# A decoder layer: the first half's attention weights stored by groups of 128 queries, and score copies shared between two engines

## The chip, the cores and the metric

The kernel runs on one core of a Trainium2 chip. The metric is the device time of one execution in microseconds (us). Three executions of the kernel before took 1036.89, 1038.47 and 1040.36 us, so its median is 1038.47 us. Besides these there is one profiled execution, which gives the page and the trace.

Engine names in the profile: PE is TensorE's matmul side and PEld its weight loads, DVE is VectorE, ACT is ScalarE, POOL is GpSimd, SP is SyncE. A name with q behind it (SPq, ACTq) is an engine's sequencer, which here issues transfers.

## The reference

The layer works on x of shape (8, 512, 256) in float32: eight batches of 512 tokens. Three blocks follow each other, each with a residual sum and a layer norm behind it.

```python
x = _layernorm(x + _L0_attn_ref(x, ...))              # windowed attention, 16 heads of 16
x = _layernorm(x + _L0_xattn_ref(x, ctx_1024, ctx_1024))  # causal cross-attention, one head
x = _layernorm(x + _L0_ffn_ref(x, ...))               # 8 experts, the best 2 for each token
```

The change lies in the first block. There each token looks at 17 keys, from 8 before it to 8 behind it, and a soft mask made from a learned width and sharpness is taken off the scores:

```python
q = _ln(silu(x @ Wq).reshape(B, L, H, D), q_g, q_b)
kv = silu(x @ Wkv)                      # k gets the same norm as q, v does not
scores = stack([einsum('blhd,blhd->blh', q, k_pad[:, w:w + L]) for w in range(K)]) * SCALE
soft_mask = sigmoid((width[..., None] - rel) * sharp[..., None])
attn = softmax(scores - (1.0 - soft_mask) * MASK_PENALTY, axis=-1)
out = sum(attn[..., w][..., None] * v_pad[:, w:w + L] for w in range(K))
```

## The kernel before, in words

**Stages.** Generators, one for each stage of a batch, are interleaved by `together` (L1110), which gives every stage a share of the iteration by costs and due times written in the code. In iteration b (L1132) the stages are `crossed(b)` (cross-attention and routing), `attended(b + 1)` (the end of the windowed attention), `scores(b + 2)` (its start) and, from iteration 1 on, some experts' tiles of 128 tokens each. A batch therefore passes through `scores`, then `attended`, then `crossed`, in three successive iterations. The first experts' tile comes in iteration 1, and the tiles that are left follow after the last batch.

**Order on the queues.** The SP queue runs its transfers in the order in which the code issues them (L83). On PE, DVE, ACT and POOL the order is planned when the kernel is built, from a model of each instruction's time; at run time each engine takes its instructions strictly in that order, and one that waits holds back all that stand behind it.

**Scores.** In `scores` (L305) q and k of one batch are computed, normed and transposed. The heads are handled in two halves, c = 0 and c = 1, of 8 heads each, and for each half in two steps `ip` of 256 queries. A step makes four tiles `pq[r]` of 128x320 numbers in PSUM from 32 small matmuls (L413): each block of 64 queries against a span of 80 keys, two heads in each of the four. The four tiles take all four buffers of their pool, so the next step's matmuls wait until they are copied out. The copies (L421) go to a tile `row` with two buffers, all four by ACT, and ACT then issues two transfers (L425) that store `row` to the DRAM array `band[c]`. The array's lines are so spaced that what is stored as blocks of 80 keys can be read back as diagonals of 17: POOL reads them into the tile `s[c]` (L387) once all stores of that half have landed.

**Weights and sums of the first three batches.** Batches below BANDED = 3 end in `summed` (L496), the others in `weighted` (L610), which uses no matmul for the sums. In `summed` DVE takes the mask off, subtracts the maximum and, after ACT's exponential, divides by the sum (L518 to L533), for c = 0 and then c = 1. Here partition p holds the queries 4p to 4p + 3. SP stores the weights of a half in one transfer, `aband<-s` (L537): 128 partitions x 4 queries x 4 pairs of heads, each a run of 34 numbers or 136 bytes. The array is laid out so that a block of 64 queries can be read back as a banded matrix over 80 keys. After the store of c = 0 SP issues the first two of eight `fetch` calls (L502), each of which reads one group g of 128 queries in two transfers `arow<-aband` (L506); the tile `arow` has two buffers. Then comes the store of c = 1, and the other six fetches follow inside the loop over groups (L567). PE transposes each `arow` (L575), DVE and ACT copy the result out as `aT` (L579), and small matmuls (L553) with the values sum it.

**What SP has behind a store.** In the iterations concerned these are the fetches, the store of the other half, the loads of x and of the context of later batches (L91, L919), and in iteration 1 the first experts' tile, whose rows `xs` (L942) come ahead of the store of batch 2 and whose weights were issued earlier still.

Of the kernel before, what the change touches and what calls it, by code (L numbers as in the profile page):

```python
# [14 lines left out]
P = 128  # L15
# [5 lines left out]
W = 17  # L21
# [4 lines left out]
HG = HH // 2  # L26
LINE = HG * SPAN * 2
HALO = W // 2
T = L // P
# [8 lines left out]
BANDED = 3  # L38
# [6 lines left out]
def decoder_layer_kernel(  # L45
# [16 lines left out]
    nc = tc.nc  # L62
# [242 lines left out]
    def scores(b, xb):  # L305
# [78 lines left out]
        def read_scores(c):  # L384
            lines = band[c].rearrange("(p t n) -> p t n", p=P, t=T)[:, :, 0:LINE]
            read.append(
                nc.gpsimd.dma_start(  # L387
                    s[c].rearrange("p t r w u -> p t r (w u)"),
                    lines.rearrange("p t (r n) -> p t r n", r=HG)[:, :, :, 0 : 2 * W],
                )  # L390
            )
# [9 lines left out]
        for c in range(2):  # L401
            s.append(apool.tile([P, T, HG, W, 2], F32, tag="s", name="s", bufs=3))
            for ip in range(T // 2):
                row = apool.tile([P, 2, HG, SPAN, 2], F32, tag="row", name="row", bufs=2)
                pq = [
                    ps_m.tile([P, 2, SPAN, 2], F32, tag="m", name=f"pq{r}") for r in range(HG)
                ]
                for ii in range(2):
                    for u in range(2):
                        at = (2 * ip + ii) * P + u * QB  # L410
                        for r in range(HG):
                            rs = slice(32 * r, 32 * r + 32)
                            nc.tensor.matmul(  # L413
                                pq[r][u * QB : (u + 1) * QB, ii],
                                qT[rs, c, at : at + QB],
                                kT[rs, c, :, at : at + SPAN].rearrange("p u k -> p k u"),
                                start=True,
                                stop=True,
                            )
                for r in range(HG):  # L420
                    nc.scalar.copy(row[:, :, r], pq[r])  # L421
                to = band[c].rearrange("(b n) -> b n", b=L // QB)[:, 0 : QB * LINE]
                to = to.rearrange("(i u) (p n) -> u p i n", u=2, n=LINE)
                for u in range(2):
                    nc.scalar.dma_start(  # L425
                        to[u, :, 2 * ip : 2 * ip + 2],
                        row[u * QB : (u + 1) * QB].rearrange("p i r k u -> p i (r k u)"),
                    )
                yield 2.0

                if c == 1 and ip == 0:
                    read_scores(0)
# [48 lines left out]
        for c in range(2):  # L481
            pc = pen[:, c].rearrange("p t r w u -> p (t r) w u")
            wc = width[:, c].rearrange("p t (r u) -> p (t r) u", u=2)
            sc = sharp[:, c].rearrange("p t (r u) -> p (t r) u", u=2)
# [11 lines left out]
    def summed(b):  # L496


        groups = [(c, g) for c in range(2) for g in range(T)]
        rows_of = {}  # L500

        def fetch(c, g):  # L502
            ar = apool.tile([P, HG, SPAN, 2], F32, tag="a", name="arow", bufs=2)
            for u in range(2):
                ub = (g * P + u * QB) * (LINE + 2)
                nc.sync.dma_start(  # L506
                    ar[u * QB : (u + 1) * QB].rearrange("p r k u -> p (r k u)"),
                    aband[c][ub : ub + QB * LINE].rearrange("(p n) -> p n", p=QB),
                )
            rows_of[c, g] = ar  # L510

        s, pen, vh = out_of.pop(b)
        for c in range(2):
            sc = s[c]


            with tc.issue_after(urgent[-1].ins) if urgent and c == 0 else nullcontext():
                nc.vector.scalar_tensor_tensor(  # L518
                    sc, pen[:, c], -4.0e4, sc, ALU.mult, ALU.add
                )  # L520
            flat = sc.rearrange("p t r w u -> p (t r) w u")
            byw = sc.rearrange("p t r w u -> p (t r) u w")
            full = [P, T * HG, W, 2]
            top = spool.tile([P, T * HG, 2], F32, tag="top", name="top")
            nc.vector.tensor_reduce(top, byw, AX.X, ALU.max)
            nc.vector.tensor_tensor(
                flat, flat, top[:, :, None, :].to_broadcast(full), ALU.subtract
            )
            nc.scalar.activation(sc, sc, AF.Exp, scale=0.25)
            den = spool.tile([P, T * HG, 2], F32, tag="den", name="den")  # L530
            nc.vector.tensor_reduce(den, byw, AX.X, ALU.add)
            nc.vector.reciprocal(den, den)
            nc.vector.tensor_tensor(  # L533
                flat, flat, den[:, :, None, :].to_broadcast(full), ALU.mult
            )
            lines = aband[c].rearrange("(p t n) -> p t n", p=P, t=T)[:, :, 0:LINE]
            nc.sync.dma_start(  # L537
                lines.rearrange("p t (r n) -> p t r n", r=HG)[:, :, :, 0 : 2 * W],
                sc.rearrange("p t r w u -> p t r (w u)"),
            )  # L540
            if c == 0:

                for early in groups[:2]:
                    fetch(*early)
            yield 5.0
        oT = apool.tile([P, KC, L], F32, tag="T", name="oT", bufs=4)
        aT = apool.tile([P, 2, HG, 2, P], F32, tag="prod", name="aT")

        def sums(c, g):
            po = ps_o.tile([P, 2, 2, QB], F32, tag="o", name="pw")  # L550
            for u in range(2):
                for r in range(HG):
                    nc.tensor.matmul(  # L553
                        po[32 * r : 32 * r + 32, u],
                        vh[c][0:SPAN, 2 * g + u, 32 * r : 32 * r + 32],
                        aT[0:SPAN, g % 2, r, :, u * QB : (u + 1) * QB],
                        start=True,
                        stop=True,
                    )

            to = oT[:, c, g * P : (g + 1) * P].rearrange("c (u q) -> c u q", u=2)
            nc.scalar.mul(to, po[:, :, 0, :], par[:, 0:1])
            nc.vector.scalar_tensor_tensor(
                to, po[:, :, 1, :], par[:, 1:2], to, ALU.mult, ALU.add
            )

        for k, (c, g) in enumerate(groups):  # L567
            if 2 <= k + 1 < len(groups):
                fetch(*groups[k + 1])
            ar = rows_of.pop((c, g))  # L570
            for i in range(2):
                pt = ps_h.tile([P, 2, 2, P], F32, tag="h", name="paT")
                for r in range(2):
                    for u in range(2):
                        nc.tensor.transpose(  # L575
                            pt[0:SPAN, r, u, :], ar[:, 2 * i + r, :, u], ident
                        )
                put = nc.scalar.copy if i else nc.vector.tensor_copy
                put(aT[0:SPAN, g % 2, 2 * i : 2 * i + 2], pt[0:SPAN])  # L579
            if k:  # L580
                sums(*groups[k - 1])
            yield 1.4
        sums(*groups[-1])
        yield 0.8
        return oT
# [546 lines left out]
    for b in range(-2, B + 1):  # L1132
        streams = [(fetched(b), 1.0, 0.45, 1.0)] if b > -2 else []
        if 0 <= b < B:
            streams.append((crossed(b), 31.0, 0.0, 0.93))
        if 0 <= b + 1 < B:
            streams.append((attended(b + 1, rows[b + 1][:, :, 0:E]), 29.4 if b + 1 < BANDED else 60.0, 0.08, 1.0))
        if b + 2 < B:
            streams.append((scores(b + 2, rows[b + 2][:, :, 0:E]), 38.0, 0.0, 0.88))
        m = max(0, -((NX * (TS - 1) - 2 * L * b) // TS)) if b < B else tiles_max  # L1140
        if m > had:
            streams.append((experts(m - had, b == B), (m - had) * 7.2, 0.0, 1.0))
            had = m
        together(*streams)
# [57 lines left out]
```

## Time and profile before

| what | value |
|---|---|
| executions | 1036.89, 1038.47, 1040.36 us |
| profiled execution, its time | 1045.55 us |
| profiled execution, its span | 1043.8 us |
| PE busy | 916.5 us (88%) |
| DVE busy | 627.4 us (60%) |
| ACT busy | 556.7 us (53%) |
| POOL busy | 251.5 us (24%) |
| mean granted TensorE clock | 0.913 |
| `aband<-s` (L537) | 6 transfers of 272 KB, at 57.8 to 220.0 us |
| `arow<-aband` (L506) | 48 transfers of 160 KB, at 67.2 to 245.2 us |
| copies `row<-pq` (L421) | 128, of 432 ns median |

All times inside an execution are counted from the start of its span. The profiled execution is 0.7% longer than the median of the three. The work that the change touches lies between 37 and 245 us: the scores of batches 0, 1 and 2 begin at about 30, 92 and 165 us, and their weights are stored from 57.8, 124.7 and 210.1 us on. PE was at work for 80% or less of many slices there and for 90% or more of nearly every slice after 300 us. A busy matmul engine is not an engine at its peak, since the durations of matmuls grow where the granted clock is low.

### The profile page before, as it was taken

What the parts mean: (1) busy time and instruction counts of PE and PEld (TensorE: products, weight loads), DVE (VectorE), ACT (ScalarE), POOL (GpSimd) and SP (SyncE); (2) the same over time, 40 slices, a digit from 0 to 9 for tenths busy, and PEclk for the clock granted to TensorE, in tenths of its full rate; (3) what the DMA queues carried; (4) which work ended last, traced back from release to release, by engine and by line L of the source; (5) the groups of instructions that cost most, each with busy time, mean ns of one, the idle gap of its engine ahead of it and who ended that gap; (6) DMA issues with size and microseconds to landing.
All of it is one profiled execution on the core that took longest, in us unless ns stands there. A gap on an engine that the chain in (4) does not pass through costs nothing. (4 is left out here: it accounts for less than half of the span.)

```text
span 1043.8 us, 18932 instructions
## 1 busy us (share of the span) xinstructions
PE 916.5 (88%) x6336; PEld 761.6 (73%) x6336; DVE 627.4 (60%) x2106; ACT 556.7 (53%) x978; POOL 251.5 (24%) x211
## 2 busy tenths in 40 slices
PE   5658879868979999999999999999999989999970
PEld 3435557546858777777888778887998988999960
DVE  5164654754489969979994989489953331111106
ACT  4556746656467556658755865576355311222224
POOL 1100100400232243125212522152241241121221
PEclk9677877867799989999999999999999999999995
DMA  9574563872699788689978896898898899999949
GB/s 205 137 124 135 115 153 81 227 164 64 185 319 311 239 267 271 198 257 337 282 206 268 309 292 184 234 364 292 264 279 256 272 260 372 314 337 323 330 116 320
DMA packets 129123, 252.09 MB, mean 242 GB/s; under 512 B 29536, under 2 KB 76704, under 8 KB 127744
## 3 DMA queue, kind: packets, MB, share of 16 engines
q1 hardware_dynamic: 89312, 183.30, 54.3%
q0 software_dynamic: 17824, 41.86, 16.2%
q10 hardware_dynamic: 21888, 25.70, 9.0%
q8 instruction: 52, 0.85, 0.3%
q14 instruction: 47, 0.39, 0.1%
HBM read 193.44 MB, written 57.36 MB: 240 GB/s over the span
## 5 line engine op out<-in xcount | busy, mean ns | idle before, releaser
L1011 PEld LDWEIGHTS ph<-xsT,w1h 128*128 128x128 f32 x2176 | 264.6, 196 | 14.2 <-issue 5.2
L1011 PE MATMUL ph<-xsT,w1h 128*128 128x128 f32 x2176 | 271.6, 280 | 2.9 <-DVE xsT L1000 2.8
L1028 PE MATMUL pf<-w2h,h 128*128 128x256 f32 x1088 | 255.9, 386 | 3.2 <-ACT h L1019 3.1
L1028 PEld LDWEIGHTS pf<-w2h,h 128*128 128x128 f32 x1088 | 204.1, 194 | 32.0 <-ACT h L1019 5.7
L1037 POOL DMA_INDIRECT total<-ye,toi x68 | 120.4, 1771 | 417.0 <-ACT ye L1036 117.0
L1019 ACT ACTIVATE h<-ph 128x512 f32<-128x512 f32 x136 | 81.2, 598 | 119.0 <-PE ph L1011 115.0
L1000 DVE COPY xsT<-pxs 128x256 f32<-128x256 f32 x68 | 28.7, 423 | 174.6 <-PE pxs L997 174.6
L651 DVE TENSOR_TENSOR prod<-prod 128x1024 f32<-128x1024 f32 (+3 forms) x160 | 104.1, 651 | 0.3
L1036 ACT ACTIVATE ye<-pf,g 128x256 f32<-128x256 f32 x68 | 32.2, 473 | 127.2 <-PE pf L1028 116.7
L643 DVE TENSOR_TENSOR prod<-vhalo,a 128x2176 f32<-128x2176 f32 x40 | 96.6, 2416 | 0.2
L815 POOL DMA_INDIRECT sorted_x<-xr,to x64 | 78.2, 1222 | 19.9 <-issue 17.1
L413 PE MATMUL pq<-kT,qT 32*64 32x160 f32 x1024 | 60.3, 391 | 19.2 <-ACT row L421 12.7
L387 POOL DMA_DIRECT2D s<-band x16 | 24.3, 1520 | 214.5 <-DMA band<-row 154.5
L321 PE MATMUL pa<-wall,xT 128*128 128x512 f32 x128 | 67.5, 615 | 6.0 <-ACT qk L323 4.7
L413 PEld LDWEIGHTS pq<-kT,qT 32*64 32x64 f32 x1024 | 37.2, 156 | 33.8 <-ACT row L421 18.1
L421 ACT COPY row<-pq 128x320 f32<-128x320 f32 x128 | 45.8, 435 | 29.4 <-PE pq L413 26.6
L575 PE MATMUL paT<-ident,arow 128*80 128x128 f32 x192 | 38.0, 346 | 20.0 <-DMA arow<-aband 17.1
L1019 ACT ACT_TABLE_LOAD x39 | 50.0, 1283 | 7.3 <-PE ph L1011 5.7
L322 PEld LDWEIGHTS pb<-wall,xT 128*128 128x128 f32 x128 | 24.2, 192 | 35.3 <-issue 23.0
L575 PEld LDWEIGHTS paT<-ident,arow 128*80 128x80 f32 x192 | 26.2, 167 | 30.8 <-issue 13.0
L711 PE MATMUL ps<-cT,x1T 128*128 128x128 f32 (+3 forms) x128 | 45.5, 476 | 0.0
L322 PE MATMUL pb<-wall,xT 128*128 128x288 f32 x128 | 41.3, 410 | 3.9 <-DVE wp L325 1.6
(196 smaller groups left out, 1392.4 us busy)
## 6 DMA issues: line engine op xcount, KB each, us to landing
w1h<-in_w_dram SPq DMA_DIRECT2D x136, 512.0 KB
w2h<-in_w_dram SPq DMA_DIRECT2D x136, 512.0 KB
band<-row ACTq DMA_DIRECT2D x64, 320.0 KB
vhalo<-vband POOLq DMA_DIRECT2D x10, 1280.0 KB, 10.1
xs<-sorted_x SPq DMA_DIRECT2D x68, 132.5 KB
arow<-aband SPq DMA_DIRECT2D x48, 160.0 KB
s<-band POOLq DMA_DIRECT2D x16, 272.0 KB, 5.8
xr<-in_x_dram SPq DMA_DIRECT2D x8, 512.0 KB
```

Source lines behind the costliest of these rows:

```text
L321: nc.tensor.matmul(pa, lhs, wall[:, kc, 0 : 2 * E], **se)
L322: turns.append(nc.tensor.matmul(pb, lhs, wall[:, kc, 2 * E :], **se))
L413: nc.tensor.matmul(pq[r][u * QB : (u + 1) * QB, ii], qT[rs, c, at : at + QB], kT[rs, c, :, at : at + SPAN].rearrange("p u k -> p k u"), st ...
L421: nc.scalar.copy(row[:, :, r], pq[r])
L575: nc.tensor.transpose(pt[0:SPAN, r, u, :], ar[:, 2 * i + r, :, u], ident)
L643: nc.vector.tensor_tensor(prod.rearrange("p w (h d) -> p w h d", d=D), vh[c][:, t : t + W, :].rearrange("p w (h d) -> p w h d", d=D), a[:, ...
L651: nc.vector.tensor_tensor(prod[:, 0:n, :], prod[:, 0:n, :], prod[:, n : 2 * n, :], ALU.add)
L815: sent = nc.gpsimd.indirect_dma_start(out=sorted_x[:, :], out_offset=bass.IndirectOffsetOnAxis(ap=to[:, n, j : j + 1], axis=0), in_=xr[:, ...
L1011: nc.tensor.matmul(ph[:, u, :], w1s[hf][:, kc, f * P : (f + 1) * P], xT[:, kc, :], start=(kc == 0), stop=(kc == KC - 1),)
L1019: nc.scalar.activation(h, ph, AF.Gelu)
L1028: nc.tensor.matmul(po, hs[fc // HU][:, fc % HU, j * P : (j + 1) * P], w2s[hf][:, f, :], start=(fc == 0), stop=(fc == NF - 1),)
L1037: add = nc.gpsimd.indirect_dma_start(out=total[:, :], out_offset=bass.IndirectOffsetOnAxis(ap=toi[:, j : j + 1], axis=0), in_=y, in_offset ...
```

## The change

Two places change.

In `scores`, for the batches 0, 1 and 2, the copies of `pq[1]` and `pq[3]` are made by DVE and those of `pq[0]` and `pq[2]` stay with ACT. The later batches keep all four on ACT.

In `summed`, the store of the weights for c = 0 is cut along the partitions into four transfers, each of 32 partitions, that is of 128 consecutive queries, so that each holds what one `fetch` reads. They are issued one after the other on SP, ahead of the first two fetches. The store for c = 1 stays one transfer. The number of runs and of bytes is the same.

```diff
                 for r in range(HG):
-                    nc.scalar.copy(row[:, :, r], pq[r])
+                    put = nc.vector.tensor_copy if b < BANDED and r % 2 else nc.scalar.copy
+                    put(row[:, :, r], pq[r])
...
             lines = aband[c].rearrange("(p t n) -> p t n", p=P, t=T)[:, :, 0:LINE]
-            nc.sync.dma_start(
-                lines.rearrange("p t (r n) -> p t r n", r=HG)[:, :, :, 0 : 2 * W],
-                sc.rearrange("p t r w u -> p t r (w u)"),
-            )
+
+            parts = T if c == 0 else 1
+            for ps in (slice(k * P // parts, (k + 1) * P // parts) for k in range(parts)):
+                nc.sync.dma_start(
+                    lines[ps].rearrange("p t (r n) -> p t r n", r=HG)[:, :, :, 0 : 2 * W],
+                    sc[ps].rearrange("p t r w u -> p t r (w u)"),
+                )
```

## The prediction, made before the result was known

> **What bounds the kernel now.** I read the page's head and slices first, then busy time by stretches, then the waits of PE and SP from 28 to 262 us, then the order of time around the stores. The page:
>
> ```profile
> PE 916.5 (88%) x6336; PEld 761.6 (73%) x6336; DVE 627.4 (60%) x2106; ACT 556.7 (53%) x978; POOL 251.5 (24%) x211
> PE   5658879868979999999999999999999989999970
> PEclk9677877867799989999999999999999999999995
> ```
>
> A slice is 26 us. From the twelfth on PE is nearly full. The first ten slices, where all that is changed lies, have idle PE and a low clock. So PE sets the end, and an idle microsecond taken from PE early moves all later work forward. By stretches (busy us of PE, PEld, DVE, ACT, POOL, then clock, DMA share, GB/s):
>
> ```profile
> 28.00:110.00 82.00, 57.63 (x517) 38.07 (x516) 32.19 (x61) 46.73 (x89) 8.10 (x8) 0.71 0.60 132
> ...
> 63.50:71.00 7.50, 0.04 (x1) 0.07 (x2) 4.32 (x8) 3.33 (x5) 0.00 (x0) 0.75 0.42 113
> ...
> 131.00:136.00 5.00, 0.15 (x2) 0.02 (x1) 0.54 (x1) 2.35 (x4) 0.00 (x0) 0.61 0.83 234
> 136.00:142.00 6.00, 5.78 (x26) 3.52 (x26) 2.01 (x6) 0.46 (x2) 0.00 (x0) 0.50 0.88 97
> ```
>
> Two stretches have no PE work at all. The waits name them (us in total, times, longest):
>
> ```profile
> PE paT L575 <- DMA arow<-aband: 17.1, 4, 7.5
> PE pq L413 <- ACT row L421: 9.1, 5, 4.8
> ```
>
> ```profile
> SPq L506 <- DMA aband<-s: 25.9, 5, 8.7
> ```
>
> PE waits for fetched weights, and SP holds the fetch until the store has landed. Batch 0 in order of time:
>
> ```profile
> 57.83 0.60 SPq L537 DMA_DIRECT2D aband<-s  x1
> ...
> 67.16 0.72 DVE L533 TENSOR_TENSOR s<-s,den 128x544 f32<-128x544 f32 x1
> 67.19 2.44 SPq L506 DMA_DIRECT2D arow<-aband  x4
> 69.80 0.63 SPq L537 DMA_DIRECT2D aband<-s  x1
> 70.93 1.50 PEld L575 LDWEIGHTS paT<-ident,arow 128*80 128x80 f32 x8 [7.92 <-DMA arow<-aband]
> 70.96 1.91 PE L575 MATMUL paT<-ident,arow 128*80 128x128 f32 x8 [7.49 <-DMA arow<-aband]
> ```
>
> The store goes out at 57.83, the fetch at 67.19, the transposes start at 70.96: 9.36 us of landing are the largest piece. The same rows put the store at 124.72 and the fetch at 131.26 in batch 1 (6.54 us, PE stall 4.85), and 210.12 and 217.51 in batch 2 (7.39 us, stall 3.08).
>
> **The change, part by part: the stores.** One transfer of 128 x 4 x 4 = 2048 runs of 136 bytes becomes four of 512. No row before shows such a quarter. The nearest is the store `wband<-wp`, 64 KB in 512 runs of 128 bytes: issued at 73.66 it lets POOL go on at 80.65 (7.0 us), at 138.70 by 144.45 (5.75), at 217.54 by 220.98 (3.44). Those are the bounds, 3.44 to 7.0. I take a line through the least of each size (512 runs 3.44, 2048 runs 6.54): 2.41 us fixed, and the rest in proportion to runs. The quarter then lands after 2.41 + (9.36 - 2.41)/4 = 4.15 us in batch 0, 3.44 in batch 1, 3.66 in batch 2, and the fetch may go 5.2, 3.1 and 3.7 us sooner. SP now issues four transfers of 0.63 us, 2.52 us in all, still under 3.44, so the landing hides the three added issues (9 in all, 5.7 us of SP). Without that cover each batch would pay up to 1.9 us. Behind them SP holds only fetches, the store of c = 1 and loads for later batches.
>
> What becomes of it on PE:
> - Batch 0: the first stall can lose 5.2 of 7.49, but group 2 is late next. Its fetch comes behind the store of c = 1, whose data are ready at 67.16 + 0.72 = 67.88 and which goes at 69.80 only because SP was issuing fetches. It can move 1.9 us, no more. The stall ahead of group 2 (1.71 us at 79.88 now) takes the rest back. I count 1.9; the other end is 5.2.
> - Batch 1: 3.1 of the 4.85. Group 2's transposes at 146.02 did not wait for a transfer, so nothing takes it back.
> - Batch 2: the stall is 3.08 and the fetch comes 3.7 sooner: 3.1. The store itself stays behind the load of `xs` on SP (209.67), which the change does not touch.
>
> Sum 8.1. With the quarter at 7.0 us it would be 1.9 + 0 + 0.4 = 2.3; at the other end 5.2 + 3.1 + 3.1 = 11.4.
>
> **The copies.** 3 batches x 2 halves x 2 steps x 2 = 24 copies leave ACT (24 x 0.432 = 10.4 us) for DVE. The trace has no DVE copy of 128x320 from PSUM. 128x256 takes 0.42 (L1000) and 80x512 takes 0.69 (L579), so by interpolation 0.49, 11.8 us in all. DVE is busy 121 of the 234 us there, so this lies beside other work unless a copy is awaited. Per step, four copies on ACT take 1.41 us; now ACT's pair (0.75) and DVE's pair (0.98) run side by side: 0.43 less. The next 32 matmuls, held by these copies, took 2.33 and where not held 1.92 (165.29): 0.41 less. On the path lies one such sum per batch, the second step's store that releases POOL's read of c = 0: 0.84 x 3 = 2.5. The first step of batch 0 stays late, since ACT reaches its copies at 37.12 only after the sigmoid at 36.10. Bounds: the whole wait of 9.1 gone on the good side. On the bad side each of 12 steps finds DVE inside its longest instruction there (0.95, L353), less the 0.43: 6.2 lost.
>
> The change adds a wait: ACT's store `band<-row` now waits for DVE too. Behind it on ACT stand `aT` copies and the `oT` scalings (L562), for which DVE (L563) and PE's sums wait.
>
> Sum 8.1 + 2.5 = 10.6, against the profiled execution's 1045.55 (span 1043.8): 1034.95, or 1.0%. That execution is 0.7% above the median of the three; on 1038.47 the same share gives 1028. What a newly planned order does to the later stages no row can tell; the range has to hold it. A difference under 0.3% (3.1 us) cannot be told from none.
>
> **Rivals.**
> - *The clock holds.* The stall in batch 1 is followed by 6 us at 0.50, and 221 to 231 us shows 0.67. Eight transposes take 1.91 us at 70.96 in such a stretch and 1.11 at 150.36 at full clock. If the shorter stalls leave the clock up, 5.78 us of PE lose 0.42 of themselves (2.4 us) and the 8.59 busy us of 221 to 231 about as much: 4.8 more, 1023. Against it: nearly every stretch before 262 us has other causes of low clock (171 to 190 us is at 0.50 with PE full). The Trainium skill (TensorE: Matmul & The Clock Gate, Part 1) says that an idle window of about 3.4 us halves the clock; by it the stalls of batches 1 and 2, 1.75 and 0, would leave it up, and the sum would be 15.4.
> - *A quarter lands hardly sooner.* If the 5.75 and 7.0 us rows are the usual ones and landing is a round trip and a queue rather than runs, the stalls stay and only the copies' 2.5 are left: 1036, no change. Against it: three whole stores of equal size differ by their company, and 3.44 has been seen. The Trainium skill (DMA: Bandwidth & Descriptors, Anatomy of one DMA) gives 2.0 us fixed plus bytes over 436 GB/s, fitted on the software path; an estimate by it is 2.64 for the whole and 2.16 for a quarter, a gain of 1.4 over three batches. The rows of 6.5 to 9.4 do not bear that out.
> - *Slower: DVE's copies stand behind a DVE instruction that itself waits.* DVE takes instructions in order; in batches 1 and 2 the sums are interleaved with the scores, and DVE waited at L563 for ACT's `oT` 20.0 us in 10 times, 2.0 each. If each of 8 steps is held so, PE's `pq` buffers and ACT's store wait 16.0 us in all; less 8.1 and batch 0's 0.8, that is 7.1 lost: 1045.5. It decides once the mean wait passes (8.1 + 0.8)/8 = 1.1 us. For it: the order on DVE is planned from a model. Against it: DVE had long idle stretches there (3.45 us before 103.42, 6.98 before 112.82, 8.73 before 180.81).
> - *The fetch waits for all four transfers*, so the change does not do what it says: three issues later in three batches, 5.7, less 2.5: 1041.7. Against it: the two stores `band<-row` at 38.53 go to interleaved parts of one array 0.6 us apart without a wait.
>
> **How the numbers follow.** Forecast 0.47 (its own range 1023 to 1034), clock 0.12, hardly sooner 0.14, DVE's wait 0.22, all four 0.05. The first two are faster; a few hundredths of them may end within the bound: faster 0.57. Hardly sooner and that rest: same 0.15. The last two: slower 0.28. The range goes from 1020, below the clock rival, to 1046, just past DVE's wait; about 0.15 lies outside, most of it where DVE waits longer than 2.0 us.
>
> **What would show it.** Right: the fetch of batch 0 goes 4 to 5 us behind the first store, the PE stalls of 4.85 and 3.08 shrink to under 2, a stall of some 5 us stands ahead of group 2 in batch 0, DVE copies take about 0.49, and the stretch from 262 us to the end keeps its length. Wrong: fetches still 6 us or more behind the store; PE or ACT waiting on DVE `row` for over 1 us a step; SP's store of c = 1 later than 69.8; or a gain before 262 us that is gone by the end because the planned order of later batches came out worse.

## The result, and the profile after

The changed kernel takes 1036.11 us (median of 14 runs, 1031.03 to 1040.22). The kernel before, run on the same chip, took 1040.28 (14 runs, 1036.39 to 1047.73). The ratio is 0.995, with a 95% interval of 0.9926 to 0.9973: faster, by half of the 1.0% that was forecast. The profiled execution took 1036.22 us with a span of 1034.5, against 1045.55 and 1043.8 before; the profiled pair is further apart (9.3 us) than the medians (4.2), so the trace is read for places, not for the sum.

The busy times and the slices, from the page of the changed kernel:

```profile
PE 903.6 (87%) x6336; PEld 753.2 (73%) x6336; DVE 639.8 (62%) x2130; ACT 549.1 (53%) x955; POOL 253.6 (25%) x211
PE   5758888679989899999999989999999988999970
PEclk9588897889889899999999999899999999999995
```

PE does the same 6336 matmuls in 903.6 us, not 916.5. Its idle time is 1034.5 - 903.6 = 130.9 us, and was 1043.8 - 916.5 = 127.3. So in this pair of executions the gain is matmuls that take less time while the granted clock is higher (0.929 over the span, 0.913 before), not fewer idle microseconds. A second profiled execution of each kernel, from the runs below, says the same of the busy time: 915.8 before, 905.5 after (idle 125.6 and 124.0).

The same holds for the part of the span in which the change lies. Up to the first expert matmul PE is busy for 195.8 us before and 183.6 after (190.9 and 184.9 in the second executions), and idle for 62.2 and 64.7 (62.7 and 64.1).

The stretches of the changed kernel: the same first one as before, then the stall of batch 0, and in batch 1 the five microseconds and the six around a new stall (the columns are us; PE, PEld, DVE, ACT, POOL busy; clock, DMA share, GB/s):

```profile
28.00:110.00 82.00, 56.50 (x539) 38.97 (x537) 40.93 (x80) 42.80 (x74) 8.10 (x8) 0.74 0.66 146
61.80:68.20 6.40, 0.07 (x1) 0.00 (x0) 6.33 (x12) 3.85 (x6) 0.00 (x0) 0.71 0.48 95
131.50:136.50 5.00, 1.88 (x22) 1.36 (x20) 4.10 (x11) 2.90 (x8) 0.00 (x0) 0.97 1.13 232
136.50:142.50 6.00, 5.46 (x34) 3.80 (x34) 1.61 (x7) 3.43 (x5) 0.57 (x1) 0.74 0.59 172
```

What PE waited for between 28 and 262 us, and SP's wait for the stores (us in total, times, longest):

```profile
PE paT L579 <- DMA arow<-aband: 14.0, 4, 6.4
PE pq L413 <- DVE row L422: 9.4, 6, 3.3
```

```profile
SPq L507 <- DMA aband<-s: 8.2, 5, 5.1
```

SP's wait for the stores is down from 25.9 us to 8.2: the change does what it says. PE's wait for the fetched weights is down by 3.1 only, from 17.1 to 14.0. PE's wait for the copies is no shorter (9.4 after and 9.1 before, 8.3 and 6.2 in the second executions), on DVE's row where it was on ACT's. The first half of the answer is in the order of time. Batch 0 and batch 1 of the changed kernel:

```profile
56.23 3.06 SPq L541 DMA_DIRECT2D aband<-s  x4
64.43 2.42 SPq L507 DMA_DIRECT2D arow<-aband  x4
67.94 0.65 SPq L541 DMA_DIRECT2D aband<-s  x1
68.27 1.91 PE L579 MATMUL paT<-ident,arow 128*80 128x128 f32 x8 [6.40 <-DMA arow<-aband]
...
78.49 1.91 PE L579 MATMUL paT<-ident,arow 128*80 128x128 f32 x8 [3.56 <-DMA arow<-aband]
...
118.66 2.63 SPq L541 DMA_DIRECT2D aband<-s  x4
121.96 2.79 SPq L507 DMA_DIRECT2D arow<-aband  x4
124.98 0.65 SPq L541 DMA_DIRECT2D aband<-s  x1
127.55 1.04 PE L579 MATMUL paT<-ident,arow 128*80 128x128 f32 x8
128.62 1.42 SPq L507 DMA_DIRECT2D arow<-aband  x2
136.59 0.41 PE L579 MATMUL paT<-ident,arow 128*80 128x128 f32 x1 [3.21 <-DMA arow<-aband]
```

In batch 0 the fetch goes 8.20 us behind the first quarter (9.36 behind the whole store before). In batch 1 it goes 3.30 us behind (6.54 before), and PE reaches the first transposes at 127.55 without a stall, where it had stalled 4.85 us up to 136.01. But group 2 of batch 1 is fetched at 128.62, as soon as the transposes of group 0 give its buffer free, 3.64 us behind the store of c = 1; it lands so that PE starts at 136.59, after a stall of 3.21. Before, the same fetch went out like this:

```profile
138.38 1.09 SPq L506 DMA_DIRECT2D arow<-aband  x2
146.02 1.24 PE L575 MATMUL paT<-ident,arow 128*80 128x128 f32 x8
```

There PE started 7.64 us behind the issue and did not wait, so this time is no landing. The landings are in the trace as well: the last piece arrived at 144.07 before, 5.69 us behind the issue (5.83 in the second execution), and at 136.50 after, 7.88 behind it (7.79). So two things make the new stall. PE was ready for group 2 only 7.64 us behind the issue before (6.03 in the second execution) and is ready after 4.76 now; and the fetch lands 2 us later. Both fetches stand behind the store of c = 1, and both land shortly after it: that store's last piece arrives at 143.37 before and at 134.10 after. Why the fetch now lands 2.4 us behind that store, not 0.7, is open.

The lead along the way, from the start times of the same instructions in two profiled executions of each kernel:

| | before | after | lead of the means |
|---|---|---|---|
| first transposes of batch 0 | 70.96, 70.82 | 68.27, 67.93 | 2.8 |
| first transposes of batch 1 | 136.01, 136.64 | 127.55, 127.97 | 8.6 |
| first gathered tokens of the experts (pxs) | 211.84, 207.82 | 207.97, 207.54 | 2.1 |
| first transposes of batch 2 | 221.52, 217.37 | 216.47, 216.54 | 2.9 |
| first expert matmul (ph) | 258.04, 253.59 | 248.30, 249.01 | 7.2 |
| from there to the end of the span | 785.8, 787.8 | 786.2, 780.5 | 3.4 |

Batch 1's lead is mostly gone by the time the experts' tokens are gathered, and something is won anew in batch 2. From batch 1's first transposes to pxs PE is idle for 8.9 and 11.2 us before, and for 19.2 and 19.5 after; the stall of 3.2 is a part of that, and the rest is not followed here. The experiments were made for these two, and for batch 0's 8.20 us.

### The profile page after: what moved, and what is told of

The parts are those of the page before. It is cut to its first block, busy times and chain, and to the rows that moved or that the text cites. A ratio compares the mean times of both kernels' runs of the same rounds, so it can differ in the third digit from the quotient of the medians.

```text
span 1034.5 us, 18962 instructions
## 1 busy us (share of the span) xinstructions
PE 903.6 (87%) x6336; PEld 753.2 (73%) x6336; DVE 639.8 (62%) x2130; ACT 549.1 (53%) x955; POOL 253.6 (25%) x211
## 5 line engine op out<-in xcount | busy, mean ns | idle before, releaser
L1004 DVE COPY xsT<-pxs 128x256 f32<-128x256 f32 x68 | 28.5, 419 | 175.2 <-PE pxs L1001 175.2
L422 ACT COPY row<-pq 128x320 f32<-128x320 f32 x104 | 37.9, 433 | 29.8 <-PE pq L413 24.7
L579 PE MATMUL paT<-ident,arow 128*80 128x128 f32 x192 | 32.0, 309 | 18.3 <-DMA arow<-aband 14.0
L689 PE MATMUL po<-c,prT 128*128 128x256 f32 x160 | 40.9, 386 | 4.3 <-ACT prT L708 4.2
L295 ACT ACTIVATE xr<-xr,off,rs 128x256 f32<-128x256 f32 x64 | 33.2, 592 | 21.2 <-DVE off L292 21.1
```

The source lines that it names most:

```text
L422: put(row[:, :, r], pq[r])
L689: nc.tensor.matmul(po, probsT[j][:, i * P : (i + 1) * P], c[:, i, :], start=(i == 0), stop=(i == j),)
```

## The experiments

All ratios are to the kernel before on the same chip, with 95% intervals. The lines of code are shown as edits of the kernel before, or of the changed kernel where it says so.

**The kernel before once more, with no edit, and the change written on as many lines as before.** The first measures the spread between equal kernels, the second the change without a shift of line numbers.

> The kernel before, unchanged, for a second profile. In the first pair of profiles the span fell by 9.3 us (1043.8 to 1034.5), the first expert matmul came 9.7 us sooner (258.04 to 248.30), PE's busy time fell by 12.9 us at the same 6336 matmuls and the rest of the span rose by 3.6. Spread: the first profile of before was a long one of its kind, and this one has its first expert matmul at about 253 and a span of about 1039. Stalls: the first expert matmul comes at 258 again, with PE waiting 17 us for fetched weights. Clock: if this profile is shorter than the first, PE's busy time falls with it (916 down to about 910) and the granted clock rises above 0.913, while the time in which PE is idle stays at 127.

> The changed kernel again, written on as many lines as before, for a second profile. Ratio 0.995 again. Stalls: PE's wait for fetched weights is again about 14 us, against 17 before, so that the stalls give 3 us and no more. Clock: PE busy about 904, idle about 131. Spread: a span of 1034 with the first expert matmul at about 248.

Measured: 0.9997 [0.9951, 1.0043] for the kernel before, 0.9924 [0.9883, 0.9966] (1032.93 us) for the change. With the first result of the change the two intervals overlap from 0.9926 to 0.9966: the change is worth some 0.5 to 0.75%. The second profile of the kernel before has its first expert matmul at 253.59, as the expectation under "Spread" has it, but PE's busy time is as long as in the first.

**Each part alone**, the stores first, then the copies.

```diff
+            parts = T if c == 0 else 1
+            for ps in (slice(k * P // parts, (k + 1) * P // parts) for k in range(parts)):
+                nc.sync.dma_start(
+                    lines[ps].rearrange("p t (r n) -> p t r n", r=HG)[:, :, :, 0 : 2 * W],
+                    sc[ps].rearrange("p t r w u -> p t r (w u)"),
+                )
```

> Only the store of c = 0 in four transfers; all copies on ACT. By the forecast's sum 8.1 us less, a ratio of 0.992. By what the profile after shows (in batch 0 the quarter landed after 8.2 us, in batches 1 and 2 after 3.3 and 2.9, and the stall moved on to group 2 by 3.6 and 3.2 us) 3 to 5 us less, 0.996. If all of it came from the copies: no change.

```diff
-                    nc.scalar.copy(row[:, :, r], pq[r])
+                    put = nc.vector.tensor_copy if b < BANDED and r % 2 else nc.scalar.copy
+                    put(row[:, :, r], pq[r])
```

> Only the copies shared between DVE and ACT; the store of c = 0 stays one transfer. By the forecast's sum 2.5 us less, 0.9976. By what the profile after shows the first store comes 1.6 us sooner, and PE's wait for the copies stays at 9 us (9.1 before, 9.4 after): about 1.5 us less, 0.9985. If the copies wait on DVE: no change or slower.

Measured: stores 0.9966 [0.9924, 1.0008] (1037.75 us), copies 0.9992 [0.9953, 1.0031] (1039.83 us). Their waits of SP for the store, the stores alone first:

```profile
SPq L506 <- DMA aband<-s: 7.1, 3, 4.9
```

```profile
SPq L506 <- DMA aband<-s: 26.7, 5, 8.9
```

The shorter wait belongs to the stores (7.1 us, against 26.7 with the copies alone). The copies bring the first store of batch 0 from 57.83 to 55.47 and that of batch 1 from 124.72 to 119.81, but that of batch 2 goes at 211.21, later than the 210.12 before: nothing of their lead is left by then.

PE's waits for fetched weights, batch by batch, in us (two figures are two executions):

| | before | stores alone | copies alone | the change |
|---|---|---|---|---|
| batch 0 | 9.2, 9.3 | 11.0 | 8.6 | 10.0, 10.3 |
| batch 1 | 4.9, 6.4 | 1.5 | 5.3 | 3.2, 3.2 |
| batch 2 | 3.1, 2.9 | 1.8 | 5.5 | 0.9, 1.5 |

The row of batch 1 is the one to read. Its second group, with the stores alone and then with the copies alone:

```profile
140.98 1.08 PE L575 MATMUL paT<-ident,arow 128*80 128x128 f32 x8 [0.23 <-DMA arow<-aband]
```

```profile
140.05 1.94 PE L575 MATMUL paT<-ident,arow 128*80 128x128 f32 x8 [2.61 <-DMA arow<-aband]
```

With the stores alone the gain stays: PE waits 1.24 us ahead of the first group and 0.23 ahead of the second. (That kernel then waits 6.44 us for ACT's `pr`, at 149.08, so it does not keep the lead either.) The stall ahead of group 2 comes with the shared copies. Where they are, PE is ready for group 2 at 8.1 to 8.4 us behind the store of c = 1, whether the store of c = 0 is cut or not; before and with the stores alone it comes at 10.4 us or later. The fetch lands 9.9 to 11.5 us behind that store in all of these profiles.

**A third buffer for the fetched weights**, on top of the change. The memory is that of a tile that only batch 3 uses.

```diff
-            ar = apool.tile([P, HG, SPAN, 2], F32, tag="a", name="arow", bufs=2)
+            ar = apool.tile([P, HG, SPAN, 2], F32, tag="o" if (c * T + g) % 3 == 2 else "a",
+                            name="arow", bufs=1 if (c * T + g) % 3 == 2 else 2)
...
-                for early in groups[:2]:
+                for early in groups[:3]:
...
-            if 2 <= k + 1 < len(groups):
-                fetch(*groups[k + 1])
+            if 3 <= k + 2 < len(groups):
+                fetch(*groups[k + 2])
```

> The change plus a third buffer for fetched weights (it takes memory that only batch 3 uses), so that the fetch of group 2 goes to SP ahead of the store of c = 1; both versions compute the same. My theory: with both parts of the change, batches 0 and 1 lose what they gained because group 2 is fetched only when a buffer comes free, and then behind the 2048 runs of the c = 1 store (stalls ahead of group 2: 4.11 and 3.24 us with both parts, 1.71 and none before). Then both stalls fall under 1.5 us, batch 1's first transposes start some 2.5 us sooner than 127.97 and the first expert matmul some 5 us sooner than 249.0: about 1028 us, ratio to before about 0.988. Rival 1: the two stalls go, but the lead is lost again in the routing on DVE before batch 2, so that the first expert matmul stays at 248 to 250 and the ratio at 0.993 to 0.995. Rival 2: a fetch in company of any other transfer lands after 5 us or more, so the stalls stay over 2.5 us whatever the order on SP.

Measured: 0.9861 [0.9829, 0.9893], 1024.99 us, the fastest kernel of this study. Batch 1 in order of time:

```profile
116.24 2.63 SPq L537 DMA_DIRECT2D aband<-s  x4
119.20 5.18 SPq L506 DMA_DIRECT2D arow<-aband  x6
125.00 0.65 SPq L537 DMA_DIRECT2D aband<-s  x1
125.78 1.04 PE L575 MATMUL paT<-ident,arow 128*80 128x128 f32 x8
131.60 0.67 PE L575 MATMUL paT<-ident,arow 128*80 128x128 f32 x4 [0.35 <-ACT aT L579]
```

The fetch at 119.20 now has six transfers, three groups, ahead of the store of c = 1 at 125.00. Group 2 starts at 131.60 and waits 0.35 us for ACT, not for a transfer. In batch 0 group 2 starts at 74.52 with no wait for a transfer, and a stall of 1.53 stands ahead of group 3. The first transposes of batch 1 come at 125.78 (127.97 with two buffers), pxs at 200.38 (207.54) and the first expert matmul at 240.29 (249.01). The stretch from batch 1's first transposes to pxs has 14.9 us of idle PE, against 19.5 with two buffers: 3.2 of the 4.6 is the stall that is gone. So the lead is not lost again in the routing (rival 1), and the stalls do go (rival 2). What cost was the late place of this fetch, after a buffer came free and behind the store of c = 1. The landings speak for the store: group 2, now ahead of it, lands 4.10 us behind its issue, and group 3, now behind it, takes 7.78. The run moves the fetch past both at once and does not part them further.

**The routing ahead of batch 2's softmax**, on the change: batch 2's first half also waits for the routing's last ordered instruction.

```diff
-            with tc.issue_after(urgent[-1].ins) if urgent and c == 0 else nullcontext():
+            with (tc.issue_after(urgent[-1].ins) if urgent and c == 0 else nullcontext(),
+                  tc.issue_after(urgent[-2].ins) if urgent[1:] and c == 0 else nullcontext()):
```

> The change, and the softmax of batch 2's first half is held behind the routing's last ordered instruction on DVE. My theory: most of batch 1's lead (8.5 us at its first transposes, 0 to 4 at the first gathered rows of the context, pxs) is lost because the planned order on DVE puts the end of the routing behind batch 2's softmax (190.4 to 191.8 us); then the scatters begin at about 189.5 instead of 192.7, pxs at about 204.5 instead of 207.5 to 208.0, the first expert matmul at 246 instead of 249, ratio to before about 0.990. Rival: the scatters wait for POOL or for the counts on TensorE, not for that place in DVE's order: pxs stays within 1 us of 207.5 and batch 2's store goes 1 to 3 us later, ratio 0.993 to 0.997.

Measured: 0.994 [0.9905, 0.9974]. The first scatter of the routed rows on POOL:

```profile
195.13 1.08 POOL L815 DMA_INDIRECT sorted_x<-xr,to  x1 [2.08 <-ACT v L324]
```

It begins at 195.13, not at 189.5, and pxs at 210.69: later than with the change alone (192.55 and 207.54). So the gain that was expected did not come. But the run does not refute the theory about this place: here the routing was already 4 us late ahead of it (DVE writes the tokens' places `to` at 189.00, against 184.97), and from there to the first scatter it takes 6.13 us, not 7.58. What holds the routing back earlier is open. With three buffers the scatters begin at 185.51 with no such edit.

**The values of the second half later**, on the change: the load of 320 KB that POOL issues ahead of the first store goes to SP, behind the store of c = 1. **And then without the read of the scores** in batch 0.

```diff
+            if b < BANDED and c == 1:
+                vh.append(vb[:, c])
+                yield 0.3
+                continue
...
+            else:
+                src = vband[b % 2][1][:, :]
+                nc.sync.dma_start(
+                    vh[1][0:SPAN],
+                    bass.AP(
+                        tensor=src.tensor, offset=src.offset,
+                        ap=[[C, SPAN], [QB * C, L // QB], [1, C]],
+                    ),
+                )
```

> The change, with the load of the second half's block of values (vblock, 320 KB, 1.5 us ahead of the first store in batch 0, on POOL's queue) moved to SP behind the store of c = 1. My theory: a quarter of 512 runs took 8.2 us in batch 0 against 2.9 to 3.3 in batch 1 because this load and the read of the scores (272 KB, at 54.6) hold the DMA engines. Without the load, store to fetch in batch 0 falls from 8.14 to 4.5 to 6 us and the first transposes start at 65 to 66 instead of 67.9; batches 1 and 2 keep their 3 to 4 us. Rival: the 8 us are the store's own way (first use of the array, a fixed queue), and they stay within 1 us of 8.14. The time of the whole: ratio 0.990 to 0.995 in both, since group 2 takes back what the first transposes gain.

```diff
+            if b == 0 and c == 1:
+                read.append(nc.gpsimd.memset(s[c], 0.0))
+                return
```

> As the run with the late values, and batch 0's read of the second half's scores (272 KB, 1.3 us ahead of the first store) is left out as well: POOL sets them to zero instead, so that half's weights in batch 0 are wrong, and the time is short of that read. My theory: the rest of the 8 us of a quarter in batch 0 is this read. Then store to fetch falls from 6.13 to 3 to 4 us, as in batches 1 and 2. Rival: the rest belongs to the store in batch 0 itself, and it stays at 5.5 us or more.

Batch 0's store and fetch, with the late values:

```profile
55.77 2.95 SPq L540 DMA_DIRECT2D aband<-s  x4
61.90 3.20 SPq L509 DMA_DIRECT2D arow<-aband  x4
66.43 1.60 PE L587 MATMUL paT<-ident,arow 128*80 128x128 f32 x8 [5.02 <-DMA arow<-aband]
```

and without the read of the scores as well:

```profile
56.73 2.71 SPq L543 DMA_DIRECT2D aband<-s  x4
59.61 4.25 SPq L512 DMA_DIRECT2D arow<-aband  x4
65.12 1.11 PE L590 MATMUL paT<-ident,arow 128*80 128x128 f32 x8 [1.20 <-DMA arow<-aband]
```

From store to fetch: 8.14 us with both neighbours, 6.13 without the values (4.5 to 6 were expected), 2.88 with neither. So the rival (the store's own way in batch 0) fell, and by more than I expected: without them the quarter lands in 2.88 us, as in batches 1 and 2. In batch 0, 5.3 of the 8.1 us go with two other transfers on POOL's queue. The whole kernel with the late values is slower, 1.012 [1.0073, 1.0167], where I expected 0.990 to 0.995. Its profile shows PE waiting 7.0 us for DVE's `aT` ahead of the sums (2.2 with the change) and 6.5 for ACT's `pr` ahead of the routing's transposes (2.3). What put those there was not tried. The time of the run without the read cannot be compared, since it leaves work out.

**Another pair of copies**: DVE has copies 0 and 2 of each four, not 1 and 3; then the same with the whole change, and with the third buffer.

```diff
-                    put = nc.vector.tensor_copy if b < BANDED and r % 2 else nc.scalar.copy
+                    put = nc.vector.tensor_copy if b < BANDED and r % 2 == 0 else nc.scalar.copy
```

> Only the copies move to DVE, stores as before, and DVE has copies 0 and 2 of each four instead of 1 and 3. The work is the same as in the run of the copies alone (ratio 0.9992, first expert matmul at 253.5); only the planned order differs. If the copies are worth what the two profiles say (nothing to 0.5%) and re-planning matters little, the ratio is 0.997 to 1.001 and the first expert matmul starts at 252 to 255. Rival: the planned order alone is worth more than the change, and this ratio differs from 0.9992 by over 0.004.

> The whole change, with DVE having copies 0 and 2 of each four instead of 1 and 3: the same work, planned anew. My theory, after the copies alone came to 0.9992 and 1.0077 with the two choices: the planned order is worth some 0.8% either way, and of the change's gain only the first groups' stalls in batches 1 and 2 are its own. Then these stalls are gone here too (store to fetch 2.8 to 3.8 us in batches 1 and 2), but the ratio may stand anywhere from 0.988 to 1.004; against the copies alone with the same choice (1.0077) it is better by 0.004 to 0.012. Rival: the choice of copies costs the 0.8% by itself (copy 0 late on DVE holds PE), and then PE's wait for DVE's row grows over 12 us from 8.3 and the ratio is 1.000 to 1.004.

> The third buffer on top of the run before this one: the change with copies 0 and 2 on DVE, and three buffers. My theory: the buffer takes away the stalls ahead of group 2 under any order, so this is better than the same kernel with two buffers by 0.004 to 0.010, and stands at 0.982 to 0.996. Rival: the 0.0139 of the first third buffer was mostly a lucky order, and here nothing or less than 0.002 is gained over two buffers.

**The third buffer alone**, on the kernel before.

> The kernel before with the third buffer for fetched weights alone: stores and copies as they were. My theory: the buffer pays because the change brought the fetch forward onto the store of c = 1; before, the stalls ahead of group 2 were 1.71 us in batch 0 and none in batch 1, so the buffer alone has at most some 2 us to give: ratio 0.996 to 1.001, the stalls ahead of the first groups stay at 7.5, 4.9 and 3.1 us. Rival: the buffer, or the order planned with it, is what gave the 0.0139, whatever the stores do: ratio under 0.993.

| ratio to before | DVE has none | DVE has 1 and 3 | DVE has 0 and 2 |
|---|---|---|---|
| stores as before | 1 | 0.9992 [0.9953, 1.0031] | 1.0077 [1.0043, 1.0111] |
| stores in four | 0.9966 [0.9924, 1.0008] | 0.995 and 0.9924 | 1.0037 [1.0001, 1.0074] |
| in four, third buffer | not run | 0.9861 [0.9829, 0.9893] | 0.992 [0.9883, 0.9957] |
| as before, third buffer | 1.0057 [1.0024, 1.009] | not run | not run |

Read down a column, the table says the same three times. The stores are worth 0.34% alone, 0.42 to 0.68% beside copies 1 and 3, and 0.40% beside copies 0 and 2. With intervals of 0.3 to 0.4% to either side, most of these differences are not clear of noise one by one; that they agree is what speaks for them. The third buffer on top gives 0.6 to 0.9% and 1.2%. Without the stores in four (and with all copies on ACT) it gives nothing: 1.0057, slower than I expected. PE's wait for the weights with the buffer alone:

```profile
PE paT L575 <- DMA arow<-aband: 16.6, 4, 7.7
```

16.6 us, as good as the 17.1 of before, with the stalls ahead of the first groups at 7.67, 5.00 and 2.85. The buffer pays where the store has been made short and the copies are shared, and not on the kernel before; with only one of the two it was not run. Why it costs 0.6% there is open.

Read across, the same work with copies 0 and 2 on DVE is slower by 0.6 to 1.1%, each time. That is as much as the whole change, or more. The rival's mechanism for it, PE held by a late copy 0, is not it: PE's wait for DVE's `row` is 9.2, 9.1 and 9.0 us with 0 and 2, and 8.1, 8.3 and 8.8 with 1 and 3. The first expert matmul comes at 265.0, 256.1 and 242.7 us against 253.5, 249.0 and 240.3, so it is lost before that point. The trace shows another planned order there; which piece of it costs is open.

## Why the prediction was right or wrong

The direction was right and the size was too large: 10.6 us were forecast, the two results for the change, 0.995 and 0.9924, are 5 to 8 us.

**The step that failed is the stores' 8.1 us, and in it the groups behind the first.** They were to come out of PE's waits for fetched weights. By themselves the stores gave 3.5 us (0.9966; the interval reaches from 7.9 gained to 0.8 lost). In the changed kernel these waits fell by 3.1 us (17.1 to 14.0), and by 3.6 in the second executions (18.6 to 15.0). Ahead of the first groups they fell by 9.0 and 9.9 us, not far from the 5.2 + 3.1 + 3.1 that the forecast had there. Ahead of the groups behind them they rose by 5.9 and 6.3, where it had 3.3, all of it in batch 0: group 2 now has a stall in each batch, of 3.56, 3.21 and 0.88 us (4.11, 3.24 and 1.46).

What then came of the 3.1 us is less still. The forecast let every idle microsecond taken from PE early move the rest forward, but other waits grew: up to the first expert matmul PE is idle for 62.2 and 62.7 us before and for 64.7 and 64.1 after. The lead of 7.2 us there is matmuls that took 9.1 us less at a higher granted clock. The forecast had left that to a rival, on top of the 8.1, so part of the right direction is luck.

**Batch 1.** The forecast counted 3.1 us there, since "Group 2's transposes at 146.02 did not wait for a transfer, so nothing takes it back". With the stores alone nothing did: the waits went from 4.85 to 1.47. In the changed kernel the stall of 4.85 at the first groups is gone, but group 2, whose fetch goes out only when a buffer comes free, behind the store of c = 1, has a stall of 3.21 us (3.24 in the second execution). That leaves 1.6 us, or 3.1 between the second executions, where the kernel before had a wait of 1.13 ahead of group 3 as well. The sum took the two parts one by one; with the copies shared PE comes to group 2 sooner behind that store than the fetch lands. The prediction looked at group 2 for batch 0 and took the order of the kernel before for batch 1. The runs with a third buffer agree: fetched ahead of that store, group 2 of batch 1 has no stall for a transfer, PE is idle for 57.4 us up to the first expert matmul, and the change with the buffer is worth 1.4%, where the change is worth 0.5 to 0.75% and the buffer by itself nothing.

**Batch 0: the net was near, the landing was not.** 1.9 us were forecast for group 2's start: it moved from 79.88 to 78.49, 1.4, and in the second executions from 79.44 to 78.96, 0.5. "group 2 is late next" held (stall 3.56 for 1.71). PE's waits there did not shrink (9.2 to 10.0 us), since it comes to both stalls sooner. The quarter was to land in 4.15 us and took 8.20, past the upper bound of 7.0: the line through the least row of each size leaves out the company. That gap goes with the two transfers of POOL's queue. The first transposes came 2.7 us sooner: 1.6 from the store going out at 56.23 (the copies' side), 1.2 from the landing. Here the rival "a quarter lands hardly sooner" was right; in batches 1 and 2, at 3.30 and 2.88 (forecast 3.44 and 3.66), it was wrong. The Trainium skill (DMA: Bandwidth & Descriptors, Anatomy of one DMA) would have, by the estimate in the prediction, 2.16 us for a quarter; without the two neighbours it took 2.88, with one 6.13, with two 8.2. The trace agrees only roughly, and only for the first. The Trainium skill's rule that each DMA engine serves the queues it has work for in turn, packet by packet (same page, Queues, rings and completion order), is the one that speaks to the neighbours, and the trace agrees with it as far as 2.88, 6.13 and 8.14 go: none, one and two other transfers.

**Batch 2: the stall of 3.08 is gone**, as forecast, and the first expert matmul comes 7 us sooner. Here the rival "the clock holds" had a part. The six microseconds from batch 2's first transposes were granted 0.50 and 0.56 before (stalls 3.08 and 2.94) and 0.51 with the third buffer alone (2.85). Without a stall they got 0.87 and 0.78 with the change, and 0.99 and 1.00 with three buffers. PE's busy time from there to the first expert matmul fell from 32.5 and 31.6 us to 28.2 and 28.5. But the stall did not lower the clock. In the kernel before it was at 0.50 some 8 us ahead of the stall (which runs from 218.44 to 221.52), behind a stretch in which PE waits for the gathered tokens and does nothing:

```profile
207.14:210.56 3.42, 0.00 (x0) 0.00 (x0) 0.48 (x1) 3.37 (x6) 0.00 (x0) 1.00 0.66 264
210.56:218.44 7.88, 4.57 (x13) 3.20 (x13) 5.19 (x19) 4.64 (x9) 0.00 (x0) 0.50 0.60 120
```

It came back at 227.63. After, it falls to 0.50 at 204.42, within the same wait, and is back at 211.25, low once more from 214.66, and up again from 218.07 for over 30 us. So the stall can at most have put off the return; no run shows that by itself, and the copies alone had a stall of 5.54 with 0.77 behind it. In batch 1 it is otherwise: there the clock falls within the stall of 4.85 before (0.50 from 132.05 to 145.71), and at the end of the new stall of 3.21 after (0.50 from 136.15 to 139.57). The Trainium skill (TensorE: Matmul & The Clock Gate, Part 1) says that an idle window of about 3.4 us halves the clock. The trace agrees for the wait for the gathered tokens, 3.42 us without PE work and then 0.50; the stalls of 2.85 to 3.08 behind it came when the clock was already low.

**The copies** were to give 2.5 us. One takes 0.49 us, as interpolated:

```profile
L422 DVE COPY row<-pq 128x320 f32<-128x320 f32 x24 | 10.8, 486 | 21.3 <-PE pq L413 15.5 <-DMA band<-row 5.8
```

By themselves they gave 0.8 us (0.9992; the interval reaches from 4.9 gained to 3.2 lost). The first stores went 2.4 and 4.9 us sooner in batches 0 and 1, and by batch 2 the lead was gone; what took it is not shown. The slower rival, DVE's copies held behind a waiting instruction, did not come: the 24 copies waited 5.8 us in all for the earlier `band<-row`, and PE's wait for `row` is 9.4 and 8.3 us where it was 9.1 and 6.2. The last rival, a fetch that waits for all four transfers, is refuted in batch 1: the fetch goes at 121.96, when by the trace the first quarter has landed (121.83) and the last lands at 126.14.

**What the range left to the plan** was rightly left: another pair of copies moves the time by as much as the change or more. (The chances of the last two rivals, 0.22 and 0.05, add up to 0.27, not 0.28.)

## What to carry to other kernels

When a transfer is made to land sooner, look at the next one on the same path even where it shows no stall: take its landing from the trace, not the start of the work behind it, and ask whether that work will still come later once everything ahead of it has moved. Two changes that look independent can meet there. The shortened store paid more once the fetch behind it had a buffer to go to; the buffer alone paid nothing. Count the busy time of the limiting engine as well as its waits: here the waits hardly fell in sum, and the matmuls got shorter. And where the instructions' order is planned anew, an edit that leaves the work the same measures what the plan alone can do.

## What was not expected of the hardware

The same store of 512 runs, 68 KB, released the fetch after 2.88 us without other company than the three quarters behind it, 6.13 beside the read of 272 KB and 8.14 beside that read and a load of 320 KB on another engine's queue. And the granted clock goes with a good part of the difference between kernels: with the same 6336 matmuls, PE was busy from 901.2 us (the stores alone, mean clock 0.928) to 918.9 (copies 0 and 2 on DVE, 0.915), while its idle time outside the matmuls went, among the kernels that leave no work out, from 119.5 (three buffers, copies 0 and 2) to 133.7 (the stores alone).
